# Layer 0's probability-value product in column halves, and layer 1's attention weights in another form, in a two-layer graph-attention kernel

## The chip, the cores and the metric

The kernel runs on one core of a Trainium2 chip. The core has a matrix engine (PE, whose weight loads the profile lists apart as PEld), a vector engine (DVE), an activation engine (ACT), a general engine (POOL) and a queue engine that starts transfers (SP). The engines run side by side, each through its own queue in order, and wait for each other through semaphores. The metric is the device time of one execution in microseconds (us). Three runs of the kernel before took 5745.4, 5747.46 and 5747.82 us; the median is 5747.46 us.

## The reference

The input is x of shape (8, 2048, 256), in float32, and one adjacency matrix of 2048 x 2048 integers, shared by all eight batches. Two layers follow each other, each with a residual and a layer norm around it.

Layer 0 is chunked attention with 4 heads of 64 features. For a head:

- the scores are q k^T / 8, clipped to the range -10 to 10, and -10 where the adjacency is 0;
- the softmax is taken inside each chunk of 256 keys, and not over all 2048;
- the result is the sum over the 8 chunks of probabilities times values, followed by an output projection, a residual and a layer norm. Outside it stand another residual and another layer norm.

Layer 1 is graph attention with 4 heads of 64 features. With Wh = h W, each node has two numbers per head, s (as the one who looks) and d (as the one who is looked at). The logit of the pair (i, j) is leaky(s_i + d_j) with slope 0.2; pairs without an edge get minus infinity; a softmax over j gives the weights, and the weighted sum of Wh goes through an elu. A residual and a layer norm end the kernel. The output is x after both layers.

Softmax does not change when a number is taken from all logits of a row. So the weights can be computed as exponentials of logits less the row's maximum, or in any form that differs from this by a factor per row.

## The kernel before

Everything lives on chip once loaded. Four slots of 128 x 4096 float32 hold, in turn, a batch's nodes, its transposed features, its queries and its keys; the next batch moves on by one slot, and its x is loaded into the slot of the transposed features (L81 issues it, SP's queue carries it) while layer 0 works. The adjacency is read once, in 16 blocks of rows. DVE makes a 0/1 block of each (L140), PE transposes it (L145), DVE writes `clipT` from it as +80 or -80 in int8 (L146), and ACT writes `edgeT` as 0 or 1 in uint8 (L149). In both, partitions are the nodes looked at, j.

A batch runs through `attention0`, `close0` and `attention1`.

`attention0` transposes the nodes (L157, copies L164 and L166), projects queries and keys (L188, copies L197 on DVE and L199 on ACT) and values (L204, L211 into `vaug`). `vaug` has 65 columns per head: 64 features and a column of ones (set at L200), so that a product with it also gives the sum of the weights. Then it loops over 2 pairs of heads and 4 chunks of 512 queries, here called a block, and inside over the 8 chunks of 256 keys. Such a key chunk is:

- `scores`: for each of its 2 tiles of 128 keys PE forms `ps` for the two heads (L234), keys on partitions, 512 queries along the free dimension. DVE clips with one pass that also applies the mask (L241: maximum with -80, minimum with `clipT`), and ACT takes the exponential of an eighth of it (L249), into `pr`.
- the product (L265): for each head of the pair, each of 4 groups of 128 queries and each of the 2 key tiles, PE loads 128 x 128 of `pr` as weights and streams the 65 columns of `vaug`, and accumulates over the two key tiles in `pc`.
- the division: DVE takes the reciprocal of the last column (L273) and multiplies (L274), and POOL adds the chunk to `acc` (L276).

The scores of chunk c+1 are issued ahead of the product of chunk c. At the end of a block, PE transposes `acc` (L280).

`close0` projects the output (L299) and does two layer norms on DVE, with POOL for the inverse square root (L177).

`attention1` transposes again, projects to Wh and to s and d in one product (`pw`, L343; ACT copies to `vaug`, L350; DVE copies to `sd`, L351). It then splits the exponential: with m the largest d of a head over all nodes, exp(leaky(s + d) - c) is, up to a factor of the row, exp(d - m) times max(exp(0.8 (s + m)), exp(-0.8 (d - m))). Both factors are numbers per node. So ACT takes exponentials of 64 numbers per partition (L371 to L373), POOL scales `vaug` by exp(d - m), ones column included (L375, L378), and a head needs one row vector over i, broadcast to all partitions: `row_of` builds it by PE transposes of a broadcast column (L328) and ACT copies (L331), four of 512 each. Per tile of 128 nodes j (16 a head), DVE then makes the whole weight tile of 128 x 2048 in one pass (L387): maximum of the row with a number per partition, times `edgeT`. PE multiplies it as weights, in halves of 64 columns of the array, with `vaug` (L393), into the bank pair `pa`. An epilogue per head copies `pa` (L404), divides (L410, L411, POOL L413), and does elu and residual (L416, L418, L419). The final layer norm and the store (L426, L429) end the batch.

A tile framework places the waits and orders each engine's queue by its own priorities; the order is fixed when the program is built. The pool `wk` has three buffers of 8 KB per partition, which `araw`, `ab`, `pr`, `tmp`, `e` and `o` share in turn. In PSUM, `psA` has two buffers of two banks (`ps`, `pa`), `psC` two (`pc`) and `psM` two (all else).

Of the kernel before, what the change touches and what calls it, by code (L numbers as in the profile page):

```python
# [8 lines left out]
F32 = mybir.dt.float32  # L9
BF16 = mybir.dt.bfloat16  # L10
I32 = mybir.dt.int32
I8 = mybir.dt.int8
U8 = mybir.dt.uint8
AF = mybir.ActivationFunctionType
ALU = mybir.AluOpType
AX = mybir.AxisListType

P = 128
# [4 lines left out]
def adj_resnorm_kernel(  # L23
# [33 lines left out]
    FAR = 100.0  # L57
# [13 lines left out]
    edgeT = big.tile([P, NT, N], U8, tag="edgeT", name="edgeT")  # L71
# [5 lines left out]
    def feats(s):  # L77
        return slots[s].rearrange("p (c n) -> p c n", n=N)
# [52 lines left out]

    nhalf = consts.tile([P, 4], F32, tag="nhalf", name="nhalf")
# [3 lines left out]
    for t in range(NT):  # L136
# [3 lines left out]
        nc.vector.tensor_scalar(ab, araw, 0, None, ALU.not_equal)  # L140
        for g in range(NT // 8):
# [7 lines left out]
            nc.scalar.copy(edgeT[:, 8 * g : 8 * g + 8, t * P : (t + 1) * P], pm)  # L149
# [30 lines left out]
    def attention0(b, xs, xt, qs, ks):  # L180
# [19 lines left out]
        nc.gpsimd.memset(vaug[:, :, :, D:D1], 1.0)  # L200
# [19 lines left out]
        for hp in range(HP):  # L220
            for q in range(NCH):
# [31 lines left out]
                for c in range(N // CHUNK):  # L253
# [7 lines left out]
                    for k in range(2):  # L261
                        pc = psC.tile([P, QT, D1], F32, tag="psC", name="pc")
                        for i in range(QT):
                            for u in range(KT):
                                nc.tensor.matmul(  # L265
                                    pc[:, i, :],
                                    lhsT=pr[:, u, k, i * P : (i + 1) * P],
                                    rhs=vaug[:, KT * c + u, 2 * hp + k, :],
                                    start=(u == 0),
                                    stop=(u == KT - 1),  # L270
                                )
# [61 lines left out]
    def attention1(b, xs, ts, us):  # L333

# [18 lines left out]
        top = small.tile([P, H], F32, tag="top", name="top")  # L355
        nc.vector.tensor_reduce(top, d, AX.X, ALU.max)
        pt = psM.tile([P, CH], F32, tag="psM", name="pt")
        nc.tensor.transpose(pt[:H, :P], top, identf)
        most = small.tile([H, 1], F32, tag="most", name="most")
        nc.vector.tensor_reduce(most, pt[:H, :P], AX.X, ALU.max)  # L360
        pb = psM.tile([P, CH], F32, tag="psM", name="pb")
        nc.tensor.matmul(pb[:, :H], lhsT=most.to_broadcast([H, P]), rhs=identf[:H, :H], start=True, stop=True)
        nc.vector.tensor_copy(top, pb[:, :H])
        topb = top.unsqueeze(2).to_broadcast([P, H, NT])
        nc.vector.tensor_sub(d, d, topb)
        nc.vector.tensor_add(s, s, topb)
        nc.vector.tensor_scalar(d, d, -FAR, None, ALU.max)
        nc.vector.tensor_scalar(s, s, FAR, None, ALU.min)
        ed = small.tile([P, H, NT], F32, tag="ed", name="ed", bufs=1)
        gd = small.tile([P, H, NT], F32, tag="gd", name="gd", bufs=1)  # L370
        nc.scalar.activation(ed, d, AF.Exp)  # L371
        nc.scalar.activation(gd, d, AF.Exp, scale=SLOPE - 1.0)
        nc.scalar.activation(s, s, AF.Exp, scale=1.0 - SLOPE)  # L373
        for t in range(NT):
            nc.gpsimd.tensor_mul(  # L375
                vaug[:, t, :, :D], vaug[:, t, :, :D], ed[:, :, t : t + 1].to_broadcast([P, H, D])
            )
        nc.gpsimd.tensor_copy(vaug[:, :, :, D], ed.rearrange("p h t -> p t h"))  # L378

        for h in range(H):  # L380
            srow = feats(ts if h % 2 else us)[:, h // 2, :]
            row_of(s[:, h, :], srow)

            pa = [psA.tile([P, 2, CH], F32, tag="psA", name=f"pa{k}") for k in range(2)]
            for t in range(NT):
                e = wkp.tile([P, N], F32, tag="wk", name="e")
                nc.vector.scalar_tensor_tensor(  # L387
                    e, srow, gd[:, h, t : t + 1], edgeT[:, t, :], op0=ALU.max, op1=ALU.mult
                )
                for i in range(NT):  # L390
                    bank, k = pa[i // 8][:, i // 4 % 2, :], i % 4
                    for z in range(2):
                        nc.tensor.matmul(  # L393
# [86 lines left out]
```

## Time and profile before

| What | Value |
|---|---|
| Median of the runs | 5747.46 us |
| The profiled execution's own time | 5745.4 us |
| Its span, first to last instruction | 5743.2 us |
| Mean granted clock of the matrix engine | 0.944 |
| Batch period (first `pw`, L343, of batch 0 to that of batch 1: 599.85 to 1304.24) | 704.4 us |
| Busy: PE, PEld, DVE, ACT, POOL | 86, 67, 66, 25, 19% |

The page's first part gives each engine's busy time and its share of the span. Its chain of work is followed back from the last instruction, at each step to what released it; the shares by engine say who set the end. A group of instructions is one line, engine, operation and tile; after the count come its total busy time and the mean of one, and behind the second bar the time that its engine stood idle just before it and who ended that. Matrix instructions overlap each other, so the mean of one is longer than the group's busy time over its count. In float32 one matmul of the program leaves two records in the trace, and counts of PE are counts of records. The timeline lists start, duration, engine, line and tile in order of time.

### The profile page before, as it was taken

What the parts mean: (1) busy time and instruction counts of PE and PEld (TensorE: products, weight loads), DVE (VectorE), ACT (ScalarE), POOL (GpSimd) and SP (SyncE); (2) the same over time, 40 slices, a digit from 0 to 9 for tenths busy, and PEclk for the clock granted to TensorE, in tenths of its full rate; (3) what the DMA queues carried; (4) which work ended last, traced back from release to release, by engine and by line L of the source; (5) the groups of instructions that cost most, each with busy time, mean ns of one, the idle gap of its engine ahead of it and who ended that gap; (6) DMA issues with size and microseconds to landing.
All of it is one profiled execution on the core that took longest, in us unless ns stands there. A gap on an engine that the chain in (4) does not pass through costs nothing.

```text
span 5743.2 us, 125328 instructions
## 1 busy us (share of the span) xinstructions
PE 4961.7 (86%) x56856; PEld 3875.7 (67%) x56856; DVE 3787.4 (66%) x5776; ACT 1426.5 (25%) x1657; POOL 1070.8 (19%) x825
## 2 busy tenths in 40 slices
PE   5998789978899788997889968899688996899967
PEld 3776667767677576775767758677586775767756
DVE  4656775567755686555865559655595556955569
ACT  2332113321133211332113320233102331123310
POOL 0112201131011311112111131111301113111131
PEclk9999899988999899998999979999799997999989
DMA  4000000000000000000000000000000000000000
GB/s 147 15 1 1 2 31 1 1 1 3 31 1 1 1 3 31 1 1 1 3 31 1 1 1 3 30 1 1 1 3 30 1 1 1 3 15 1 1 1 17
DMA packets 39010, 60.45 MB, mean 11 GB/s; under 512 B 1616, under 2 KB 36432, under 8 KB 36432
## 3 DMA queue, kind: packets, MB, share of 16 engines
q1 hardware_dynamic: 35712, 50.34, 2.6%
q8 instruction: 448, 7.34, 0.5%
q10 hardware_dynamic: 2768, 2.10, 0.1%
q14 instruction: 82, 0.67, 0.0%
HBM read 35.65 MB, written 16.78 MB: 9 GB/s over the span
## 4 chain that ended last, share of the span: by engine, by line
PE 68%; DVE 21%; POOL 7%; issue 3%; ACT 1%; DMA 0%; POOLq 0%; ACTq 0%; DVEq 0%
PE pc L265 33%; PE ps L234 17%; DVE e L387 10%; PE pa L393 8%; PE pp L188 4%; POOL vaug L375 2%; PE pw L343 2%; PE pv L204 2%; POOL acc L276 1%; POOL hh L413 1%; DVE pr L241 1%; DVE tmp L310 1%; DVE tmp L313 1%; PE pt L280 1%; PE pt L157 1%
## 5 line engine op out<-in xcount | busy, mean ns | idle before, releaser
L265 PEld LDWEIGHTS pc<-vaug,pr 128*128 128x128 f32 x16384 | 1867.1, 192 | 382.1 <-issue 339.6
L265 PE MATMUL pc<-vaug,pr 128*128 128x65 f32 x16384 | 1936.6, 277 | 0.0
L249 ACT ACTIVATE pr<-pr 128x1024 f32<-128x1024 f32 x1024 | 1082.4, 1057 | 2069.4 <-DVE pr L241 2036.2
L241 DVE SCALAR_TENSOR_TENSOR pr<-ps,clipT 128x1024 f32<-128x1024 f32 x1024 | 1210.4, 1219 | 315.3 <-PE ps L234 308.8
L387 DVE SCALAR_TENSOR_TENSOR e<-slot,gd,edgeT 128x2048 f32<-128x2048 f32 x512 | 1195.9, 2392 | 94.5 <-PE pa L393 56.7
L393 PE MATMUL pa<-vaug,e 128*64 128x65 f32 x32768 | 1089.6, 227 | 169.8 <-DVE e L387 100.1
L393 PEld LDWEIGHTS pa<-vaug,e 128*64 128x64 f32 x32768 | 1028.1, 142 | 236.2 <-DVE e L387 156.2
L234 PE MATMUL ps<-slot,slot 64*128 64x512 f32 x4096 | 1106.2, 620 | 29.3 <-DVE pr L241 29.3
L276 POOL TENSOR_TENSOR acc<-acc,part 128x512 f32<-128x512 f32 x448 | 568.6, 1269 | 2902.6 <-DVE part L274 2902.6
L273 DVE RECIPROCAL rd<-pc 128x4 f32<-128x4 f32 x1024 | 187.3, 183 | 872.2 <-PE pc L265 872.2
L234 PEld LDWEIGHTS ps<-slot,slot 64*128 64x128 f32 x4096 | 364.9, 185 | 348.9 <-issue 135.7
L274 DVE TENSOR_TENSOR part<-pc,rd 128x256 f32<-128x256 f32 x896 | 380.3, 424 | 63.7 <-DVE rd L273 3.2
L413 POOL TENSOR_TENSOR hh<-raw,dn 128x512 f32<-128x512 f32 x64 | 123.9, 1935 | 1178.4 <-DVE dn L410 871.3
L404 ACT COPY raw<-pa 128x520 f32<-128x520 f32 x64 | 37.9, 593 | 988.5 <-PE pa L393 988.5
L299 PE MATMUL po<-wo_sb,slot 128*128 128x256 f32 x512 | 159.0, 482 | 111.5 <-DVE tmp L306 111.5
L157 PE MATMUL pt<-identf,slot 128*128 128x128 f32 x512 | 106.7, 361 | 166.4 <-DVE slot L318 87.9
L299 PEld LDWEIGHTS po<-wo_sb,slot 128*128 128x128 f32 x512 | 125.5, 251 | 143.5 <-DVE tmp L306 120.2
L157 PEld LDWEIGHTS pt<-identf,slot 128*128 128x128 f32 x512 | 76.7, 178 | 192.4 <-issue 94.8
L188 PE MATMUL pp<-slot,wq_sb 128*128 128x512 f32 x256 | 128.4, 655 | 77.6 <-DVE slot L164 68.4
L375 POOL TENSOR_TENSOR vaug<-vaug,ed 128x256 f32<-128x256 f32 x128 | 123.3, 1004 | 190.4 <-ACT ed L371 190.4
L166 ACT COPY slot<-pt 128x512 f32<-128x512 f32 x64 | 37.1, 580 | 478.6 <-PE pt L157 478.5
L188 PEld LDWEIGHTS pp<-slot,wq_sb 128*128 128x128 f32 x256 | 51.8, 210 | 149.3 <-DVE slot L164 74.2
(78 smaller groups left out, 2343.5 us busy)
## 6 DMA issues: line engine op xcount, KB each, us to landing
slot<-in_x_dram SPq DMA_DIRECT2D x8, 2048.0 KB, 8.5
araw<-in_adj_dram SPq DMA_DIRECT2D x16, 1024.0 KB, 4.8
out_dram<-o SPq DMA_DIRECT2D x32, 512.0 KB, 2.9
wq_sb<-in_wqT_dram ACTq DMA_DIRECT2D x1, 256.0 KB, 5.9
wk_sb<-in_wkT_dram ACTq DMA_DIRECT2D x1, 256.0 KB, 8.0
wv_sb<-in_wvT_dram ACTq DMA_DIRECT2D x1, 256.0 KB, 8.8
wo_sb<-in_woT_dram ACTq DMA_DIRECT2D x1, 256.0 KB, 9.7
w_sb<-in_w_dram ACTq DMA_DIRECT2D x1, 256.0 KB, 9.0
```

The source lines that it names most:

```text
L157: nc.tensor.transpose(pt[:, k * P : (k + 1) * P], src[:, q * QT + k, c * P : (c + 1) * P], identf,)
L188: nc.tensor.matmul(pp, lhsT=w[:, kc, c * P : (c + 1) * P], rhs=xT[:, kc, q * CH : (q + 1) * CH], start=(kc == 0), stop=(kc == KC - 1),)
L234: nc.tensor.matmul(ps[:, k, :], lhsT=kT[rows, hp, t * P : (t + 1) * P], rhs=qT[rows, hp, cols], start=True, stop=True,)
L241: nc.vector.scalar_tensor_tensor(pr[:, u], ps, -CLIP, clipT[:, t, cols].unsqueeze(1).to_broadcast([P, 2, CH]), op0=ALU.max, op1=ALU.min,)
L249: nc.scalar.activation(pr[:, u], pr[:, u], AF.Exp, scale=0.125)
L265: nc.tensor.matmul(pc[:, i, :], lhsT=pr[:, u, k, i * P : (i + 1) * P], rhs=vaug[:, KT * c + u, 2 * hp + k, :], start=(u == 0), stop=(u == ...
L274: nc.vector.tensor_mul(part[:, k], pc[:, :, :D], rd.to_broadcast([P, QT, D]))
L276: nc.gpsimd.tensor_add(accv, accv, part)
L299: nc.tensor.matmul(po[:, k, :], lhsT=cT[:, c, t * P : (t + 1) * P], rhs=wo_sb[:, c, :], start=(c == 0), stop=(c == KC - 1),)
L375: nc.gpsimd.tensor_mul(vaug[:, t, :, :D], vaug[:, t, :, :D], ed[:, :, t : t + 1].to_broadcast([P, H, D]))
L387: nc.vector.scalar_tensor_tensor(e, srow, gd[:, h, t : t + 1], edgeT[:, t, :], op0=ALU.max, op1=ALU.mult)
L393: nc.tensor.matmul(bank[z * D : (z + 1) * D, k * D1 : (k + 1) * D1], lhsT=e[:, i * P + z * D : i * P + (z + 1) * D], rhs=vaug[:, t, h, :], ...
```

## The change

Two things are changed, in the two layers.

In layer 0, each product of probabilities and values (L265) with 128 queries as weights is issued as two products with 64 queries, each to its own half of the partitions of `pc`, and so on its own half of the array's columns.

In layer 1 the split of the exponential is replaced by logits less each row's maximum. `vaug` is filled with ones once at the start and not scaled. Instead of `edgeT`, ACT keeps `mask`, the adjacency with the looking nodes i on partitions. For each head a row of d over j is built (`drow`), shifted to be at least 1, and for each tile of 128 nodes i one fused DVE operation multiplies it with the mask and takes the maximum along the row (L366 after the change). From s and this maximum DVE forms `gg`, so that with `s8` = 0.8 s and `d8` = -0.8 d the logit less its row's maximum is max(s8_i, d8_j) + gg_i + d_j. A head needs two rows, of `s8` and of `gg`. Per tile of nodes j DVE forms max(s8, d8) + gg (L396), then bounds it by 1e30 times `clipT`, which sends pairs without an edge far down (L400), and ACT takes the exponential with d as the bias (L401). PE multiplies with `vaug` as weights and the tile as the moving operand, in four products of 512 columns, into a transposed result of 65 x 2048 (L403). The epilogue copies it (L412), transposes it back in 16 pieces (L419), and divides and finishes in four groups on DVE, with ACT for the exponential (L422 to L431).

```diff
-    FAR = 100.0
+    FAR = 1e30
...
-    edgeT = big.tile([P, NT, N], U8, tag="edgeT", name="edgeT")
+    mask = big.tile([P, NT, N], U8, tag="mask", name="mask")
...
+    nc.gpsimd.memset(vaug, 1.0)
...
+        nc.scalar.copy(mask[:, t, :], ab)
...
-            nc.scalar.copy(edgeT[:, 8 * g : 8 * g + 8, t * P : (t + 1) * P], pm)
...
-        nc.gpsimd.memset(vaug[:, :, :, D:D1], 1.0)
...
-                                nc.tensor.matmul(
-                                    pc[:, i, :],
-                                    lhsT=pr[:, u, k, i * P : (i + 1) * P],
-                                    rhs=vaug[:, KT * c + u, 2 * hp + k, :],
-                                    start=(u == 0),
-                                    stop=(u == KT - 1),
-                                )
+                                for z in range(2):
+                                    half = slice(z * D, (z + 1) * D)
+                                    nc.tensor.matmul(
+                                        pc[half, i, :],
+                                        lhsT=pr[:, u, k, i * P + z * D : i * P + (z + 1) * D],
+                                        rhs=vaug[:, KT * c + u, 2 * hp + k, :],
+                                        start=(u == 0),
+                                        stop=(u == KT - 1),
+                                    )
...
-        top = small.tile([P, H], F32, tag="top", name="top")
...
-        nc.scalar.activation(ed, d, AF.Exp)
-        nc.scalar.activation(gd, d, AF.Exp, scale=SLOPE - 1.0)
-        nc.scalar.activation(s, s, AF.Exp, scale=1.0 - SLOPE)
-        for t in range(NT):
-            nc.gpsimd.tensor_mul(
-                vaug[:, t, :, :D], vaug[:, t, :, :D], ed[:, :, t : t + 1].to_broadcast([P, H, D])
+        most = small.tile([P, H, NT], F32, tag="most", name="most", bufs=1)
+        low = small.tile([P, H], F32, tag="low", name="low", bufs=1)
+        for h in range(H):
+            drow = wkp.tile([P, N], F32, tag="wk", name="drow")
+            row_of(d[:, h, :], drow)
+            nc.vector.tensor_reduce(low[:, h : h + 1], drow, AX.X, ALU.min)
+            nc.vector.tensor_scalar(drow, drow, low[:, h : h + 1], 1.0, ALU.subtract, ALU.add)
+            for t in range(NT):
+                scr = small.tile([P, N], BF16, tag="scr", name="scr", bufs=1)
+                nc.vector.tensor_tensor_reduce(
+                    out=scr,
+                    in0=drow,
+                    in1=mask[:, t, :],
+                    scale=1.0,
+                    scalar=0.0,
+                    op0=ALU.mult,
+                    op1=ALU.max,
+                    accum_out=most[:, h, t : t + 1],
+                )
+            nc.vector.tensor_scalar(
+                most[:, h, :], most[:, h, :], low[:, h : h + 1], -1.0, ALU.add, ALU.add
             )
-        nc.gpsimd.tensor_copy(vaug[:, :, :, D], ed.rearrange("p h t -> p t h"))
...
+        nc.vector.tensor_scalar(s8, s, 1.0 - SLOPE, None, ALU.mult)
+        nc.vector.tensor_scalar(d8, d, SLOPE - 1.0, None, ALU.mult)
+        nc.vector.tensor_add(most, most, s)
+        nc.vector.scalar_tensor_tensor(most, most, SLOPE, most, op0=ALU.mult, op1=ALU.max)
+        nc.vector.scalar_tensor_tensor(gg, s, SLOPE, most, op0=ALU.mult, op1=ALU.subtract)
...
-            srow = feats(ts if h % 2 else us)[:, h // 2, :]
-            row_of(s[:, h, :], srow)
-
+            sg = feats(ts if h % 2 else us)
+            srow, grow = sg[:, 0, :], sg[:, 1, :]
+            row_of(s8[:, h, :], srow)
+            row_of(gg[:, h, :], grow)
...
                 nc.vector.scalar_tensor_tensor(
-                    e, srow, gd[:, h, t : t + 1], edgeT[:, t, :], op0=ALU.max, op1=ALU.mult
-                )
...
+                    e, srow, d8[:, h, t : t + 1], grow, op0=ALU.max, op1=ALU.add
+                )
+
+                nc.vector.scalar_tensor_tensor(e, clipT[:, t, :], FAR, e, op0=ALU.mult, op1=ALU.min)
+                nc.scalar.activation(e, e, AF.Exp, bias=d[:, h, t : t + 1])
+                for q in range(NCH):
+                    nc.tensor.matmul(
+                        pa[q // 2][:D1, q % 2, :],
+                        lhsT=vaug[:, t, h, :],
+                        rhs=e[:, q * CH : (q + 1) * CH],
+                        start=(t == 0),
+                        stop=(t == NT - 1),
+                    )
+            hT = wkp.tile([D1, N], F32, tag="wk", name="hT")
+            for k in range(2):
                 nc.scalar.copy(
...
+                    hT[:, 2 * k * CH : 2 * (k + 1) * CH], pa[k][:D1].rearrange("p a n -> p (a n)")
+                )
+            for g in range(NT // 4):
+                ph = psM.tile([P, 4, D1], F32, tag="psM", name="ph")
+                for k in range(4):
+                    t = 4 * g + k
+                    nc.tensor.transpose(ph[:, k, :], hT[:, t * P : (t + 1) * P], identf[:D1, :D1])
...
+                nc.vector.tensor_mul(hh, ph[:, :, :D], dn.to_broadcast([P, 4, D]))
```

Lines after the change are numbered some two lines higher up to `close0`: L265 becomes L267, L273 becomes L275, L188 becomes L189, L328 and L331 (`row_of`) become L330 and L333, L157 and L164 become L158 and L165.

## The prediction, made before the changed kernel was run

> **What bounds the kernel now.** I read the page's busy times first, then its chain, then the costliest groups, then the timeline of one chunk of layer 0 and of one head of layer 1.
>
> ```profile
> PE 4961.7 (86%) x56856; PEld 3875.7 (67%) x56856; DVE 3787.4 (66%) x5776; ACT 1426.5 (25%) x1657; POOL 1070.8 (19%) x825
> ...
> PE 68%; DVE 21%; POOL 7%; issue 3%; ACT 1%; DMA 0%; POOLq 0%; ACTq 0%; DVEq 0%
> ...
> L265 PE MATMUL pc<-vaug,pr 128*128 128x65 f32 x16384 | 1936.6, 277 | 0.0
> L241 DVE SCALAR_TENSOR_TENSOR pr<-ps,clipT 128x1024 f32<-128x1024 f32 x1024 | 1210.4, 1219 | 315.3 <-PE ps L234 308.8
> L387 DVE SCALAR_TENSOR_TENSOR e<-slot,gd,edgeT 128x2048 f32<-128x2048 f32 x512 | 1195.9, 2392 | 94.5 <-PE pa L393 56.7
> L393 PE MATMUL pa<-vaug,e 128*64 128x65 f32 x32768 | 1089.6, 227 | 169.8 <-DVE e L387 100.1
> ```
>
> PE sets the end overall, but the two layers differ. A group ends in "busy us, mean ns of one", and a count is of records: a float32 matmul leaves two. L265 is 1936.6 / 16384 = 118 ns a record with a full-width weight load; L393, the same 65 moving columns on half the array's columns, is 1089.6 / 32768 = 33 ns.
>
> In the timeline one chunk of layer 0 goes like this (columns: start, duration, engine, line):
>
> ```profile
> 505.60 3.79 PE L265 MATMUL pc<-vaug,pr 128*128 128x65 f32 x32
> 507.64 0.18 DVE L273 RECIPROCAL rd<-pc 128x4 f32<-128x4 f32 x1 [0.35 <-PE pc L265]
> 507.93 0.43 DVE L274 TENSOR_TENSOR part<-pc,rd 128x256 f32<-128x256 f32 x1
> 509.32 1.99 PE L234 MATMUL ps<-slot,slot 64*128 64x512 f32 x8
> 509.43 0.18 DVE L273 RECIPROCAL rd<-pc 128x4 f32<-128x4 f32 x1 [1.07 <-PE pc L265]
> ```
>
> PE has no hole: 3.72 us of pc, then 1.91 us of ps, a period of 5.63 us, while the window of that period shows DVE 3.56 and ACT 2.11 us. PE is the bound here. In a head of layer 1 DVE is:
>
> ```profile
> 622.02 7.83 DVE L387 SCALAR_TENSOR_TENSOR e<-slot,gd,edgeT 128x2048 f32<-128x2048 f32 x3 [4.46 <-ACT slot L331]
> 633.51 12.70 PE L393 MATMUL pa<-vaug,e 128*64 128x65 f32 x384 [8.21 <-POOL vaug L378]
> 682.96 27.23 DVE L387 SCALAR_TENSOR_TENSOR e<-slot,gd,edgeT 128x2048 f32<-128x2048 f32 x12
> 703.45 2.09 PE L393 MATMUL pa<-vaug,e 128*64 128x65 f32 x64 [0.17 <-DVE e L387]
> ```
>
> Twelve passes back to back take 27.23 us, 2.27 us each; PE needs 2.12 us per tile (12.70 / 6) and waits 0.17 to 0.18 us for each.
>
> [...]
>
> **The change, part by part.** Units are one batch (8 of them), 8 layer-0 blocks (2 head pairs x 4 query chunks) of 8 key chunks, and 4 heads of 16 tiles.
>
> *Layer 0, halves.* Per key chunk 32 records of 118 ns become 64. Nearest row: L393, 12.70 / 384 = 33.1 ns, so 2.12 us for 3.72. ps stays, so PE's period is 1.91 + 2.12 = 4.03 us. DVE's own needs are 3.56 us busy and some 0.25 us of dependent gaps, so PE still leads, by little. The probabilities are done in time: ACT ends the next chunk's exponentials about 4.7 us after its ps begin, its pc starts at 4.03 + 1.91. A block takes 48.58 us now (435.74 to 484.32). Eight chunks give 12.8 us; I take off 0.8 for the seam between blocks, where DVE's four passes and POOL's last sum were covered by the longer pc. 12.0 x 64 = 768 us saved. Bounds: 640 (DVE leads, period 4.35) to 820 (nothing lost).
>
> *Layer 1, what goes.* From the first pw (599.85) to the next batch's first pp (797.32) is 197.5 us, and from there to 857.0, just ahead of that batch's first pc (858.51), 59.7; together 257.2. In it are POOL's scaling of vaug (15.4), one DVE pass per tile, and PE's halves.
>
> *Layer 1, what comes*, on DVE, in order of its queue:
> 1. pw as now, 15.5; then the first row: 4 transposes and a copy, four times, as 618.07 to 622.0 now: 3.9.
> 2. Row maxima: per head a reduction of 2048 (estimate 2.28 from L125's 416 ns at 256, at 1.04 ns an element), a subtract of 2048 (1.22, L140), small ones; 15 for four. Then 64 fused passes. Each is a pass like L387 (2.34) and a readout of the accumulator (a tiny operation, 0.15 as L176), and each waits for the one in front: 2.5 us, 160. POOL, ACT and PE have nothing beside it: all of it is path. Bounds 2.35 to 2.7; half rate, 4.65, is a rival.
> 3. gg's small operations and its row: 5.1, DVE idle.
> 4. The weights: two passes per tile in place of one. 2.34 + 2.27, of which the second reads what the first wrote; such a pair shows a gap of 0.04 (rd to part at 509.43) where independent ones overlap by 0.07. 4.62 x 64 = 296. Under it ACT's exponential runs (1.06 at 1024 elements, L249, so 1.91 at 2048[...]) and PE's four matmuls of 512 columns: L188's run at 107.18 is 27.47 us for 64 records, 0.43 each, 3.43 per tile. Both fit under 4.62, and a tile of e is free after about 10.3 us where three buffers allow 13.9. Uncovered, PE would cost only if its clock falls (below).
> 5. Seams. DVE's queue holds a head's whole epilogue ahead of the next head's first pass, and PE's and ACT's queues hold the next head's two rows behind the epilogue. So after the last pass: exponential 2.1, matmuls to the first copy 2.0, copy of 1024 (1.03), transposes 1.1; then the 24 epilogue operations of DVE, whose fourth exponential ends 13.1 us after the last pass; then seven row copies on ACT, 5.7 to 6.3 us (625.7 - 618.75 for eight now). 19.5 between heads, three times: 58.5. Bounds 14 and 23.
> 6. The last head's epilogue, norms on DVE (four groups at 3.7 us, as 5727.01 to 5730.70) and the next batch's four transposed copies queued behind these; those transposes can't start before, since both halves of that slot carry rows now. 28 us, where 6.4 passes now from the last pass (790.92). The next projections then meet no norms and take what the first batch took, 48.5 (105 to about 153.7, ahead of its first pc at 154.28).
>
> Sum: 15.5 + 3.9 + 160 + 15 + 5.1 + 296 + 58.5 + 28 + 48.5 = 630.5 for 257.2: 373.3 more, x 8 = 2986 us.
>
> *Setup.* 16 mask copies of 2048 on ACT for 32 of edgeT at 1012 ns, one memset of vaug on POOL: nothing; PE's transposes and DVE's passes of the adjacency (period 4.61 at 87.86 to 92.48) hide them. Uncovered, some 15 us. DMAs are the same, on the same queues.
>
> Total against the profiled execution: 5743.2 - 768 + 2986 = 7961 span, with its 2.2 us around it 7963. Its 5745.4 is the lowest of the three; their median is 2 higher. Forecast 7963.
>
> **Rivals.**
> - *Half rate of the fused pass.* 2.15 us more x 512 = 1100: 9060.[...] 8 in 100.
> - *PE becomes the bound of the weights.* PE stands idle for the 175 us of maxima, and at 46% busy it was granted 0.68 (540 to 600, 27.54 of 59.85 us). At half clock its 3.43 would be 6.9 us a tile, 2.2 over DVE: 64 x 2.2 x 8 = 1130, so 9090. Against it: it would be 74% busy, and layer 1 holds 0.95 now. 4 in 100.
> - *The halves gain little in layer 0*: alternating tile shapes with ps every chunk, or DVE at the lead, leave below 300 us of the 768: 8500 to 8730. Against it, ps already has another shape than pc, and DVE's 3.8 is under 5.63. 4 in 100.
> - *Not slower.* The one way is that the added passes cost little: 8 x (c - 257.2) = 768 needs c = 353.2 a batch; all that isn't the three passes is 174.5, which leaves 178.7 / 64 = 2.79 us for three passes, 0.93 each. It decides at 0.93 us, and the quickest 2048-element pass on the page with only one tensor to read takes 1.22 (L140). 1 in 100.
>
> **How the numbers follow.** My sum has 83 in 100. Its ends: fused pass 2.35, pair 4.54, seams 14, tail 22, layer 0 at 820 give about 7620; fused 2.7, pair 4.75, seams 23, tail 32, layer 0 at 640 give about 8300. All these ends together are unlikely; 7660 to 8380 holds all but 3 of the 83, with room for a seam or a clock that I mis-sized upward. That is 8 in 10. The half rate, the clock and the lost halves lie outside. This kernel can be told from no change at about 0.2%, 11.5 us: slower by more than that has 0.985, within it 0.005, faster 0.01.
>
> **What would show it.** Layer 0's period per chunk: 4.03 us, pc records at 33 ns, and DVE and PE both near 95% busy. Fused passes at 2.3 to 2.4 us each with a readout after each; PE idle beside them for 175 us a batch. L396 and L400 at 4.6 us a pair with ACT at 2 us and PE at 3.4 us a tile under them. About 19 us without a long DVE pass between heads. DVE, not PE, heads the chain, with well over half. The forecast fails if a fused pass takes over 4 us, if PE's clock in the weights is near a half, or if the seams are hidden after all.

## The result, and the profile after

The changed kernel takes 7855.78 us, the median of four runs (7854.82 to 7859.9), beside 5747.64 us for the kernel before on the same chip: a ratio of 1.3669, with a 95% interval of 1.3645 to 1.3692. The forecast was 7963 us in 7660 to 8380, so the sign was right and the time 1.4% too high. The profiled execution took 7854.82 us; its span is 7853.0 us, 2109.8 more than before, and the mean granted clock of the matrix engine fell from 0.944 to 0.839.

The page of the changed kernel, in its busy times, its chain and its costliest groups:

```profile
PE 5282.2 (67%) x46080; PEld 2779.2 (35%) x46080; DVE 6220.3 (79%) x7904; ACT 2635.4 (34%) x2449; POOL 824.0 (10%) x618
...
DVE 45%; PE 43%; ACT 5%; issue 4%; POOL 3%; DMA 0%; ACTq 0%; DVEq 0%; POOLq 0%
...
L403 PE MATMUL pa<-e,vaug 128*65 128x512 f32 x4096 | 2011.8, 649 | 659.6 <-ACT e L401 652.0
...
L396 DVE SCALAR_TENSOR_TENSOR e<-slot,d 128x2048 f32<-128x2048 f32 x512 | 1191.3, 2346 | 238.7 <-ACT slot L333 141.5
...
L366 DVE CUSTOM_DVE_ANT_0 scr<-drow,mask 128x2048 bf16<-128x2048 f32 x512 | 1172.5, 2290 | 15.2
L400 DVE SCALAR_TENSOR_TENSOR e<-clipT,e 128x2048 f32<-128x2048 int8 x512 | 1160.7, 2287 | 8.8
...
L267 PE MATMUL pc<-vaug,pr 128*64 128x65 f32 x32768 | 1082.2, 224 | 24.6 <-DVE rd L275 22.8
```

Three DVE groups of 512 passes, 1161 to 1191 us each, stand where L387 stood with 1196: the two added ones, L366 and L400, are 2333 us of DVE's busy time. On the other side, L267 has twice the records of L265 and takes 1082.2 us for 1936.6.

In the timeline a key chunk of layer 0 now reads (start, duration, engine, line):

```profile
351.71 2.09 PE L267 MATMUL pc<-vaug,pr 128*64 128x65 f32 x64
353.73 1.99 PE L234 MATMUL ps<-slot,slot 64*128 64x512 f32 x8
354.97 2.36 DVE L241 SCALAR_TENSOR_TENSOR pr<-ps,clipT 128x1024 f32<-128x1024 f32 x2 [0.41 <-PE ps L234]
355.64 0.74 PE L267 MATMUL pc<-vaug,pr 128*64 128x65 f32 x18
```

From one start of pc to the next it is 3.93 us (351.71 to 355.64) where it was 5.63: 2.02 for 64 records, 31.6 ns each, and 1.91 for ps. PE is busy in all of it, and DVE waits 0.41 us for ps: PE still bounds the chunk. A block, from one transpose of `acc` to the next, takes 35.57 us for 48.58.

In the phase of the row maxima DVE is alone:

```profile
534.80 2.29 DVE L366 CUSTOM_DVE_ANT_0 scr<-drow,mask 128x2048 bf16<-128x2048 f32 x1
537.02 0.08 DVE L366 DVE_READ_ACCUMULATOR2_ANT most<- 128x1 f32 x1
537.14 2.29 DVE L366 CUSTOM_DVE_ANT_0 scr<-drow,mask 128x2048 bf16<-128x2048 f32 x1
```

A fused pass and its read-out come every 2.34 us. Between two heads of the weights DVE stands still twice:

```profile
755.63 2.29 DVE L400 SCALAR_TENSOR_TENSOR e<-clipT,e 128x2048 f32<-128x2048 int8 x1
765.80 0.16 DVE L422 TENSOR_SCALAR dn<-ph 128x4 f32<-128x4 f32 x1 [7.87 <-PE ph L419]
...
776.71 4.61 DVE L396 SCALAR_TENSOR_TENSOR e<-slot,d 128x2048 f32<-128x2048 f32 x2 [4.39 <-ACT slot L333]
```

Here it waits 7.87 us for the first transposed sums, has 6.3 us of epilogue, small gaps, and waits 4.39 us for the next head's rows: 18.8 us without a long pass.

Term by term, for one batch, in us (means over the batches; the times in brackets are batch 0's, whose first `pw` starts at 496.93):

| Term | forecast | measured |
|---|---|---|
| Layer 0 with its close, against before | -96 | -102.4 (342.9 from first pc to first pw, for 445.3) |
| pw and the first row, to the first reduction (515.54) | 19.4 | 18.6 |
| row maxima | 175 | 163.1 |
| gg and its row | 5.1 | 5.0 |
| weights, four heads | 296 | 303.1 |
| three seams | 58.5 | 55.2 |
| tail, to the next pp (1042.65 to 1076.07: 33.4) | 28 | 31.0 |
| next projections, to the first pc (1124.41: 48.3) | 48.5 | 49.0 |
| all of the last seven rows; before | 630.5; 257.2 | 625.0; 258.3 |

Over the kernel, layer 0 gave 819 us (768 forecast) and layer 1 took 2929 (2986 forecast): 51 and 58 make up the 108 us by which the sum was too high.

### The profile page after: what moved, and what is told of

The parts are those of the page before. It is cut to its first block, busy times and chain, and to the rows that moved or that the text cites. A ratio compares the mean times of both kernels' runs of the same rounds, so it can differ in the third digit from the quotient of the medians.

```text
span 7853.0 us, 107020 instructions
## 1 busy us (share of the span) xinstructions
PE 5282.2 (67%) x46080; PEld 2779.2 (35%) x46080; DVE 6220.3 (79%) x7904; ACT 2635.4 (34%) x2449; POOL 824.0 (10%) x618
## 4 chain that ended last, share of the span: by engine, by line
DVE 45%; PE 43%; ACT 5%; issue 4%; POOL 3%; DMA 0%; ACTq 0%; DVEq 0%; POOLq 0%
DVE scr L366 15%; PE pc L267 12%; PE ps L234 11%; DVE e L396 11%; PE pa L403 10%; DVE e L400 7%; ACT e L401 4%; PE pp L189 3%; DVE pr L241 3%; PE pb L330 2%; PE pw L344 2%; PE pv L204 1%; POOL acc L278 1%; DVE low L362 1%; DVE tmp L312 1%
## 5 line engine op out<-in xcount | busy, mean ns | idle before, releaser
L403 PE MATMUL pa<-e,vaug 128*65 128x512 f32 x4096 | 2011.8, 649 | 659.6 <-ACT e L401 652.0
L401 ACT ACTIVATE e<-e,sd 128x2048 f32<-128x2048 f32 x512 | 1025.4, 2003 | 1468.7 <-DVE e L400 1468.7
L249 ACT ACTIVATE pr<-pr 128x1024 f32<-128x1024 f32 x1024 | 1083.0, 1058 | 1259.5 <-DVE pr L241 1226.9
L396 DVE SCALAR_TENSOR_TENSOR e<-slot,d 128x2048 f32<-128x2048 f32 x512 | 1191.3, 2346 | 238.7 <-ACT slot L333 141.5
L403 PEld LDWEIGHTS pa<-e,vaug 128*65 128x65 f32 x4096 | 589.4, 149 | 2062.0 <-issue 1178.0
L366 DVE CUSTOM_DVE_ANT_0 scr<-drow,mask 128x2048 bf16<-128x2048 f32 x512 | 1172.5, 2290 | 15.2
L400 DVE SCALAR_TENSOR_TENSOR e<-clipT,e 128x2048 f32<-128x2048 int8 x512 | 1160.7, 2287 | 8.8
L267 PEld LDWEIGHTS pc<-vaug,pr 128*64 128x64 f32 x32768 | 1004.0, 138 | 414.8 <-issue 362.3
L267 PE MATMUL pc<-vaug,pr 128*64 128x65 f32 x32768 | 1082.2, 224 | 24.6 <-DVE rd L275 22.8
L330 PE MATMUL pb<-identf,gg 128*128 128x128 f32 x512 | 97.0, 349 | 892.1 <-DVE gg L386 887.9
L333 ACT COPY slot<-pb 128x512 f32<-128x512 f32 x256 | 146.5, 585 | 938.0 <-PE pb L330 936.9
L330 PEld LDWEIGHTS pb<-identf,gg 128*128 128x128 f32 x512 | 73.8, 179 | 914.2 <-issue 889.9
L330 PE MATMUL pb<-identf,sd 128*128 128x128 f32 x512 | 85.3, 302 | 342.0 <-ACT drow L333 336.0
L275 DVE RECIPROCAL rd<-pc 128x4 f32<-128x4 f32 x1024 | 178.0, 174 | 150.4 <-PE pc L267 150.4
L158 PE MATMUL pt<-identf,slot 128*128 128x128 f32 x512 | 128.6, 422 | 240.1 <-DVE slot L320 87.9
```

The source lines that it names most:

```text
L249: nc.scalar.activation(pr[:, u], pr[:, u], AF.Exp, scale=0.125)
L267: nc.tensor.matmul(pc[half, i, :], lhsT=pr[:, u, k, i * P + z * D : i * P + (z + 1) * D], rhs=vaug[:, KT * c + u, 2 * hp + k, :], start=(u ...
L330: nc.tensor.transpose(pb[:, k * P : (k + 1) * P], col[:, t : t + 1].to_broadcast([P, P]), identf)
L366: nc.vector.tensor_tensor_reduce(out=scr, in0=drow, in1=mask[:, t, :], scale=1.0, scalar=0.0, op0=ALU.mult, op1=ALU.max, accum_out=most[:, ...
L396: nc.vector.scalar_tensor_tensor(e, srow, d8[:, h, t : t + 1], grow, op0=ALU.max, op1=ALU.add)
L400: nc.vector.scalar_tensor_tensor(e, clipT[:, t, :], FAR, e, op0=ALU.mult, op1=ALU.min)
```

## Experiments

**The halves alone.** The first part of the change in the kernel before:

```diff
-                                nc.tensor.matmul(
-                                    pc[:, i, :],
-                                    lhsT=pr[:, u, k, i * P : (i + 1) * P],
...
+                                for z in range(2):
+                                    half = slice(z * D, (z + 1) * D)
+                                    nc.tensor.matmul(
+                                        pc[half, i, :],
+                                        lhsT=pr[:, u, k, i * P + z * D : i * P + (z + 1) * D],
```

> The kernel before with one part of the change alone: layer 0's product in halves; layer 1 as before. Theory A, the two parts of the change do not touch each other: in the trace after, the first pw of a batch comes 102.7 us earlier (497.14 against 599.85), so 8 x 102.7 = 822 us go, 4926 us. Theory B, the parts help each other (layer 1 after leaves PE idle, and PE then has full clock in the next batch's layer 0): the halves alone then meet a busier PE, the clock falls below 1.00 in layer 0, and the gain is clearly less, my own term of 768 or under it: 4980 us or more.

4932.4 us, ratio 0.8584 (0.857 to 0.8599), so 813.6 us less than before. In the changed kernel layer 0 gave 819 us; so the parts of the change add up to within 6 us, and theory B is out. A block takes 35.57 us here too.

**One half after the other.**

```diff
-                        for i in range(QT):
-                            for u in range(KT):
-                                for z in range(2):
+                        for z in range(2):
+                            for i in range(QT):
+                                for u in range(KT):
```

> As the halves alone, but with the loop over the two halves outermost: 16 matmuls for queries 0 to 63 of each 128, all on one half of the columns, then 16 on the other half. Same instructions, same operands, other order. Theory A, the gain comes from neighbouring matmuls on different halves of the columns whose weight loads and streams run side by side: in this order neighbours share a half, so a record goes from 31.6 ns towards the 118 ns of the full width or at least to 60, pc from 2.02 us to 3.8 or more for 64 records, a chunk to 5.7 us or more; about 1.8 x 8 x 64 = 900 us over the halves alone, 5800 us and perhaps more than the kernel before. Theory B, a load of 64 columns is simply so much shorter than one of 128 that order plays no part: same as the halves alone, 4926 us.

5551.25 us, 619 more than the halves alone. The timeline:

```profile
352.00 3.41 PE L267 MATMUL pc<-vaug,pr 128*64 128x65 f32 x64
355.35 1.99 PE L234 MATMUL ps<-slot,slot 64*128 64x512 f32 x8
```

64 records now take 3.35 us, 52 ns each, with the same instructions and operands. So the order matters, but my lower bound of 60 ns was too high: two records of 64 columns one after the other (104 ns) are a little cheaper than one of 128 (118). Of the 1.70 us that a chunk gains, 1.33 belong to neighbours on different halves, 0.37 to the shape. The starts of the single records in the two traces show the pairing (medians): with the halves alone a record on the other half starts 7 ns after its neighbour, and the next pair follows 52 ns later. One half after the other, a record starts 58 ns after the one before it, whether both sum into the same place of `pc` or not, so repeated sums into one place are not what costs; only where the half changes, after every 16 records (8 products), do some start 2 to 6 ns apart.

**Quarters.** `range(4)` and 32 queries in place of `range(2)` and 64.

> As the halves alone, but in quarters of 32 queries, each on its own 32 columns of the array: 128 records for each chunk's pc in place of 64. Theory A, neighbours run side by side, and more tiles give more of it: a record goes to about 16 ns, pc at or under 2.0 us, and the chunk stays at 3.9 or falls to DVE's limit of about 3.8: 4860 to 4930 us. Theory B, at 31.6 ns a record PE is at the pace at which it can issue: the record stays at about 32 ns, pc takes 4.1 us, the chunk 6.0: (6.0 - 3.93) x 512 = 1060 us over the halves alone, about 5990 us.

4973.78 us, 41 more than the halves alone: theory A's record and chunk, but neither theory's time. Its group and its timeline:

```profile
L267 PE MATMUL pc<-vaug,pr 128*32 128x65 f32 x65536 | 1087.9, 221 | 106.5 <-issue 78.4
```

```profile
387.49 2.02 PE L267 MATMUL pc<-vaug,pr 128*32 128x65 f32 x128
389.44 1.99 PE L234 MATMUL ps<-slot,slot 64*128 64x512 f32 x8
```

A record does go to 15.2 ns (1.95 us for 128), so PE was not at the pace of its issue, and a chunk to 3.87 us. But twice the records at half the time give next to nothing: a chunk's product takes 1.95 us for 2.02, and 512 chunks at 0.06 are 31 us. And PE now has holes ahead of these products, 78.4 us in all, in which it waits for nothing that the profile shows; blocks take from 34.84 to 40.28 us, with the halves 35.57 for the most part. The program's instruction transfers grew from 9.44 to 13.63 MB; whether the holes have to do with that, no run shows.

**Less DVE and POOL in layer 0.** In the halves alone:

```diff
-                        nc.vector.tensor_mul(part[:, k], pc[:, :, :D], rd.to_broadcast([P, QT, D]))
+                        nc.vector.tensor_mul(
+                            part[:, k, : QT // 2 if c else QT],
...
-                        nc.gpsimd.tensor_add(accv, accv, part)
+                        nc.gpsimd.tensor_add(accv[:, :, : QT // 2], accv[:, :, : QT // 2], part[:, :, : QT // 2])
```

> As the halves alone, with work of DVE and POOL left out: for key chunks 1 to 7 only half of each scaled product is formed and summed (the multiplication of pc by rd and POOL's sum, queries of two of the four tiles left out). PE's work is unchanged. It takes 2 x about 0.21 us from DVE's 3.4 us busy in a chunk. Theory A, PE bounds layer 0 after the halves (it has 3.93 of 3.93 us busy in a chunk): less than 30 us change from the halves alone. Theory B, DVE's chain of passes sets the pace and PE's records only stretch to fill it: 0.3 to 0.4 us a chunk go, 150 to 200 us in all.

4868.19 us, 64 less: between the two. The trace splits it. Starts of pc are still 3.93 us apart (347.60, 351.53): inside a block PE bounds, as theory A has it. But a block is 34.76 us for 35.57, and that 0.81 lies at its end. PE waits there for POOL's last sum before it can transpose `acc`, 1.09 us with the halves alone and 0.41 here; and ahead of the last chunk's product it waits until DVE has read the buffer of `pc` that this product is to fill, 0.36 us and 0.23.

**The last sum on DVE.**

```diff
-                        nc.gpsimd.tensor_add(accv, accv, part)
+                        eng = nc.vector if c == N // CHUNK - 1 else nc.gpsimd
+                        eng.tensor_add(accv, accv, part)
```

> The run with the halves alone, with the sum of a block's last key chunk on DVE in place of POOL. It asks what holds the 0.6 us that a block of layer 0 loses at its end: with less work of DVE and POOL left in a block, 64 us went, and of that PE's wait for POOL's last sum ahead of the transposes of acc fell from 1.09 to 0.42 us. Theory A, the last sum is on the path: on DVE 512 elements take about 0.7 us (0.42 at 256) for POOL's 1.27 and a hand-over less, so the transposes start 0.5 to 0.76 us earlier: 32 to 49 us less than the halves alone, 4885 to 4900 us. Theory B, DVE is the path there: its sum stands ahead of the next block's passes over ps, which then come later by what PE gains: within 10 us of the halves alone, 4932.

4892.38 us, ratio 0.8516 (0.8502 to 0.853), 40 less than the halves alone. A block takes 34.96 us, the sum 0.69 for POOL's 1.27, and PE's wait ahead of the transposes is 61.3 us in all for 101.4, which is the gain:

```profile
359.26 0.65 PE L283 MATMUL pt<-identf,acc 128*128 128x128 f32 x4 [0.48 <-DVE acc L279]
```

Theory A holds: the last sum is on the path. But this is not what a block loses by the change. In the kernel before, PE waits for POOL's last sum as well (90.6 us in all; one such wait is the first line below). What is new is the wait ahead of the last product, which the kernel before doesn't have (second and third line, from the changed kernel, at one block's end):

```profile
490.25 0.66 PE L280 MATMUL pt<-identf,acc 128*128 128x128 f32 x4 [1.08 <-POOL acc L276]
```

```profile
358.09 0.34 PE L267 MATMUL pc<-vaug,pr 128*64 128x65 f32 x4 [0.36 <-DVE rd L275]
...
363.53 0.66 PE L282 MATMUL pt<-identf,acc 128*128 128x128 f32 x4 [1.09 <-POOL acc L278]
```

Of the versions that leave no work out, this is the fastest that ran here: it keeps the first part of the change and leaves layer 1 as before.

**The rows ahead.** In the changed kernel:

```diff
-        for h in range(H):
+        def rows(h):
             sg = feats(ts if h % 2 else us)
...
+        ahead = rows(0)
+        for h in range(H):
+            srow, grow = ahead
+            if h + 1 < H:
+                ahead = rows(h + 1)
```

> The changed kernel with one thing moved: the two rows of head h + 1 are built (transposes on PE, copies on ACT) ahead of head h's passes, not behind head h's epilogue; their slot is free, since heads alternate between two. Theory A, my item 5: a seam between heads is serial work in queue order, and the rows are its last part, 4.39 us in which DVE waits for the last row copy (757.92 to 776.71 in all). They vanish under the passes: 24 seams x 4.4 = 105 us less than the changed kernel, about 7750 us; a seam goes from 18.8 to 14.4 us. Theory B, DVE would have to wait for something else at that place, PE's clock or the matmuls of the head: under 30 us less.

7647.08 us, ratio 1.3297 (1.3275 to 1.332): 209 less than the changed kernel, twice what theory A had. DVE's waits, first of the changed kernel, then with the rows ahead (what waits, for what, total, times, longest):

```profile
DVE dn L422 <- PE ph L419: 234.6, 32, 9.2
...
DVE e L396 <- ACT slot L333: 141.5, 32, 4.8
...
DVE e L396 <- PE pa L403: 86.2, 71, 2.1
```

```profile
DVE dn L428 <- PE ph L425: 138.2, 56, 6.1
DVE e L402 <- PE pa L409: 107.8, 77, 4.3
...
DVE e L402 <- ACT slot L333: 33.6, 8, 4.2
```

The wait for rows lost 107.9 us, which is my 105. Another 96.4 came off the other wait of the seam, and 21.6 came back as waits for a buffer; the rest of the 209 lies in no wait that this view lists. Once the rows are issued early, the framework's fixed order puts the next head's first passes into the epilogue: one ahead of it, and the next between the first divisions, at 767.37.

```profile
763.36 2.35 DVE L402 SCALAR_TENSOR_TENSOR e<-slot,d 128x2048 f32<-128x2048 f32 x1 [4.28 <-PE pa L409]
```

So the order that I had taken for a fixed rule of the queue came with the late rows.

**Two tiles ahead.**

```diff
+            if h + 1 < H:
+                early = {t: weights(h + 1, t) for t in range(2)}
             for g in range(NT // 4):
```

> As the run with the rows ahead, and besides the weights of the next head's first two tiles (two passes on DVE and one exponential on ACT each) are issued ahead of the epilogue. Theory A: DVE has these 9.25 us of passes where it now waits. The buffer of tile 14 comes free at about 761.5, so its first pass runs from there to 766.2, the second to 770.8, the epilogue's 6.3 us follow, and tile 2 starts at about 777 where it now starts 28 us after the last pass (18.8 + 9.25 = 28.05 against 19.2): 24 x 8.9 = 212 us less than the changed kernel, about 7640. Theory B, the exponentials ahead of the epilogue's small ones on ACT and the matmuls behind its transposes on PE only move the wait to the first tiles of the next head: no less than the run with the rows ahead, about 7750 or more.

7620.32 us, ratio 1.3253 (1.3233 to 1.3273): 235 below the changed kernel, close to the 212, but only 27 below the run with the rows ahead. Theory A's total was met by other steps than its own: passes already ran in the seam with the rows alone, and the two tiles, priced at 107 beyond the rows' 105, gave 27.

**Half of the products.** Even tiles' products left out:

```diff
-                for q in range(NCH):
+                for q in range(NCH if t % 2 else 0):
```

> The changed kernel with half of layer 1's products of weights and values left out: only odd tiles enter PE's sum; DVE's and ACT's work on all tiles stays. PE then needs 1.97 us a tile for 3.93. Theory A, PE is covered by DVE's 4.63 us a tile except where it shows as a wait: 86 us in which DVE waits for PE to free a buffer of e, and at each head's end what of the last two tiles' 7.86 us of matmuls runs beyond the last exponential plus one tile, about 1.6 us, 32 x 1.6 = 51: 137 us less, about 7720 us. Theory B, the weights are PE's after all (the clock that is granted in them is 0.89, and the chain runs along PE for a good part of a head): the passes come closer together within a head, below 4.5 us a pair, and far more than 200 us go. Theory C, with PE idle for longer the clock falls further and the epilogues, the norms and the next projections take longer: less than 60 us go.

7752.44 us, 103 less, between theories A and C. From first to last pass the 32 heads take 2289.3 us for 2424.9, 135.6 less. That is near theory A's 137 by chance: A had 86 of it inside the heads and 51 at their ends. Inside the heads DVE's waits for PE (86.2) and for the exponential (10.7) are gone, and about 30 us come from the passes themselves; at the ends nothing was gained, for the seams grew from 441.6 to 470.2, theory C's part. The windows of the passes of the first head show PE's side (columns: window, length, then busy us of PE, PEld, DVE, ACT and POOL, then the granted clock):

```profile
685.20:756.72 71.52, 39.79 (x56) 10.53 (x56) 71.52 (x32) 30.03 (x15) 0.00 (x0) 0.71 0.00 0
```

For the changed kernel:

```profile
683.56:757.92 74.36, 54.15 (x111) 15.89 (x112) 72.42 (x32) 30.05 (x15) 0.00 (x0) 0.89 0.00 0
```

With half the work PE's busy time is still 73% of the changed kernel's in this head (39.79 us for 54.15) and 66% over all 32 (36.9 us for 55.8), at a granted clock of 0.71 for 0.89 here, and of 0.76 for 0.87 over all. The low clock then reaches into the seams. A tile's eight records take 3.65 us at a granted clock of 1.00 (746.58 in the changed kernel); behind the second head's last exponential they took 6.47 here, at 0.56. And DVE's wait for the first transposed sums rose from 234.6 us to 261.9, 27 of the 28.6:

```profile
849.08 6.47 PE L403 MATMUL pa<-e,vaug 128*65 128x512 f32 x8 [3.58 <-ACT e L401]
```

```profile
DVE dn L422 <- PE ph L419: 261.9, 32, 9.1
```

DVE has no hole left in a head: 71.52 us for 16 tiles, 4.47 a tile, is what the two passes cost by themselves. Theory B had this sign, under 4.5 us a pair, but not the 200 us with it.

**Four buffers.**

```diff
-    wkp = ctx.enter_context(tc.tile_pool(name="wk", bufs=3))
+    wkp = ctx.enter_context(tc.tile_pool(name="wk", bufs=4))
...
+            scr = wkp.tile([P, N], BF16, tag="wk", name="scr")
             for t in range(NT):
-                scr = small.tile([P, N], BF16, tag="scr", name="scr", bufs=1)
```

> The changed kernel with four buffers of 8 KB in the pool of e in place of three (the fused pass's scratch output lies in that pool too, to make room). Theory A, the 86 us in which DVE waits for PE to free a buffer are a matter of buffering: PE needs 3.93 us a tile at the clock it gets and DVE 4.63, so PE catches up later in the head: 60 to 90 us less than the changed kernel, about 7780. Theory B, PE's last tile does not come earlier by it, so the wait only moves to the head's end, where DVE waits for the transposed sums: under 20 us less.

7672.89 us, ratio 1.3355 (1.3335 to 1.3374): 183 less, twice theory A's. The heads lost 136.3 us, to 71.52 each, the same floor as with half of the products, though PE has all of its work here; so either cure, less work for PE or one more buffer, removes the waits. DVE no longer waits for a buffer of e, and its passes come in pairs (two of L396, two of L400) all through a head, so that no pass follows the one whose result it reads, as half of the 512 second passes do in the changed kernel; the two groups are 25 us less busy. The maxima lost 52.2 us, 156.5 a batch for 163.1, which I had not meant to touch. Two runs follow that up.

**The scratch, once a head.** In the changed kernel, the line of `scr` moved ahead of the loop over t.

> The changed kernel with one edit: the scratch output of the fused pass is taken from its pool once a head, not once a pass (same buffer, three buffers for e as before). In the run with four buffers 183 us went where 60 to 90 were expected; in its profile the heads are 136.3 us shorter in all, and the phases of the maxima 52.2 us, with a fused pass every 2.213 us in place of 2.337. Theory A, the second part is the scratch: taking a buffer anew makes each pass wait for the release of the pass in front, 0.124 us: 512 x 0.124 = 63, of which 52 showed; about 52 us less than the changed kernel, 7804. Theory B, it came with the fourth buffer (a row of the next head that is there earlier): the pass stays at 2.337 us, under 10 us less.

7880.04 us, ratio 1.3715 (1.3692 to 1.3738), 24 more than the changed kernel; a fused pass still comes every 2.34 us. Theory A fell. The 24 are mainly in the heads (2443.0 us for 2424.9), which the edit doesn't touch. They go with PE's clock: 15 of the 32 heads take over 77 us here, 7 in the changed kernel, and in each of these the granted clock is 0.82 to 0.85, while the others, at 76.1 or less, have 0.87 to 0.89. Why other heads have the low clock here, is open.

**Two scratches.**

```diff
-                scr = small.tile([P, N], BF16, tag="scr", name="scr", bufs=1)
+                scr = small.tile([P, N], BF16, tag="scr", name="scr", bufs=2)
```

> The changed kernel with two scratch buffers for the fused pass in place of one, taken anew in each pass as before; three buffers for e. Taking the one scratch once a head changed nothing in a fused pass (2.337 us still), so the 2.213 us of the run with four buffers came from something else. Theory A: there two scratches were live, the passes of two heads took turns, and neighbours wrote to different buffers; what costs 0.124 us is that a pass waits for the pass in front to have written the buffer that both use. Then two buffers do the same: 2.213 us a pass, 512 x 0.124 = 63 us at most and 52 as seen there, so 50 to 65 us less than the changed kernel, about 7800. Theory B, the wait is on something else that two heads do not share (the row, the accumulator's read-out into the same small tile): still 2.337 us and under 10 us less.

7800.31 us, ratio 1.357 (1.3548 to 1.3593), 55 less. In the timeline:

```profile
534.72 2.29 DVE L366 CUSTOM_DVE_ANT_0 scr<-drow,mask 128x2048 bf16<-128x2048 f32 x1
536.93 0.08 DVE L366 DVE_READ_ACCUMULATOR2_ANT most<- 128x1 f32 x1
536.93 2.29 DVE L366 CUSTOM_DVE_ANT_0 scr<-drow,mask 128x2048 bf16<-128x2048 f32 x1
```

A pass every 2.21 us, and the next one starts with the read-out and not 0.12 us after it. Theory A holds: a pass that writes the buffer which the pass in front wrote waits for it, on one engine too. In both traces each such pass waits for a semaphore that the read-outs raise. With one buffer it starts some 0.03 us after the end of the read-out in front. So by its timing the cost is that of a wait which the framework places; what two passes into one buffer would cost without it, no run shows.

**Half of the maxima.**

```diff
+        nc.gpsimd.memset(most, 1.0)
...
-            for t in range(NT):
+            for t in range(0, NT, 2):
```

> The changed kernel with half of the row maxima left out: the fused multiply-and-maximum runs for the even tiles only, the others' maxima are set to 1.0. Theory A, my item 2: DVE alone carries the phase and nothing runs under it, so 32 passes x 2.337 us x 8 batches = 598 us go, 7257 us, to within 10. Theory B, part of the phase hides work that shows when it is shorter (copies, the clock, row copies that wait): clearly less than 598, 500 or under. Theory C, the idle phase costs PE its clock in what follows: more than 598 goes, since the weights and the tail behind it then run at a higher clock.

7274.94 us, 581 less. The phases themselves are 88.4 us for 163.1, 597.6 in all, so nothing runs under them. 17 us come back elsewhere, more than the 10 I allowed, and 14 of them are in the heads (2439.1 us for 2424.9): 12 of the 32 take over 77 us, where 7 did.

## Why the prediction was right, point by point

The mechanism was right in both layers: PE's product set layer 0's pace, and three passes of DVE set layer 1's. That the total is off by only 1.4% is partly luck: over the kernel the forecast of the maxima was 95 us too high and that of the weights 57 too low, and within the weights two errors cancel.

- *Layer 0, halves*: the mechanism was right, the term mis-sized by 51 us. I took the new record from a group's busy time over its count (33.1 ns, and the page shows 33.0 again), but in a run of 64 a start-to-start distance counts, 31.6 ns; the old 3.72 us was such a distance. So the period is 3.93 and not 4.03. The loss at a block's end is real and was 0.6 us, not 0.8 (8 x 1.70 = 13.6 against 13.01). Its place was half right: the traces put it at the wait for DVE's reading of `pc` ahead of the last product (0.36 us, none before), and not at POOL's last sum, for which PE waits about as long in the kernel before (1.08 us and 1.09). No run takes DVE's part away alone. "DVE and PE both near 95% busy" was wrong for DVE: 3.38 of 3.93 us, 86%.
- *Item 2, the maxima*: all of it is path, as half of the maxima showed. The fused pass took 2.34 us, just below my lower bound of 2.35: I counted the read-out at 0.15, and it is 0.08 and overlaps. 0.16 x 512 = 82 of the 95 us. Without its read-out the pass, which the trace lists as a custom operation, takes 2.29 us for 2048 elements of a float32 row and a uint8 mask, where L387, with the same kinds of sources, has a median of 2.34. So the half rate did not occur; the trace of the kernel before had no such pass for it or against it, and the rival that was worth 1100 us fell. The reduction of 2048 took the 2.28 us of my estimate (L362, 2281 ns; with L125's 416 at 256 that is 1.04 ns an element).
- *Item 4, the weights*: 296 forecast, 303.1 measured, two errors of opposite sign. The two passes alone are 4.47 us a tile, not 4.62; I priced each second pass as one that follows its own source, and half of them are interleaved in pairs. And PE did cost: without its hold on the buffers the heads lose 136 us, 86 of them waits for it and most of the rest passes that come in pairs. I had allowed 13.9 us for a tile of e against 10.3 needed. What failed is the PE price at full clock: 3.43 us a tile became 3.93 at a granted 0.87, and tiles reach ACT at uneven distances, two and two. ACT's exponential, 1.91 us by my estimate from L249, took 2.00. The rival that PE becomes the bound stayed small.
- *Item 5, the seams*: 18.4 us on average for 19.5, but not by the steps. From the last exponential to PE's first result it is 3.85 us for my 2.0 in the seam shown, since PE is behind by more than one tile there (12 records are left, a tile has 8); the epilogue and the rows are shorter. The queues do hold the order that I gave, but it isn't fixed: with the rows ahead the passes move into the epilogue by themselves.
- *Item 6, the tail*: 31.0 for 28 (33.4 in batch 0), the same late PE result (6.2 to 9.2 us of waiting ahead of the last epilogue) beside a clock of 0.65 in batch 0; their shares were not separated. The next projections were right to 0.5 us.
- *The chain*: I expected DVE ahead "with well over half". It has 45% and PE 43%, since the 343 us a batch of layer 0 are still PE's.
- *Not slower* was excluded by the passes: three of them take 6.8 us a tile, and it would have needed 2.79.
- *The sums of the ends*: the upper ends named add up to 8376 us, not to about 8300, so the range had no room above them; and the rival of the lost halves begins at 7963 + 468 = 8431, not at 8500. Neither decided anything.

## What to carry to other kernels

A change that helps PE where PE bounds (here 814 us) can still come with a larger loss: two added passes over every element, on the engine that bounds the other stage, cost 2929 us with the seams and the tail around them, and no repair of seams and buffers that was tried, each alone, got back more than 235 of it. Price a record in a burst by the distance of starts, price PE at the clock that it gets in a stage with as many holes (0.87 in these heads, 0.76 with half of their products), and let neighbouring instructions alternate, between halves of the array on PE (31.6 ns a record for 52) and between output buffers on DVE (2.21 us a pass for 2.34). Before you call a seam serial by queue order, ask which late input put the order there.

## What the runs showed of the hardware that I had not expected

- The same 64 records take 2.02 us in alternating column halves, where neighbours start 7 ns apart, and 3.35 us one half after the other, where they start 58 ns apart; quarters go to 15.2 ns a record but gain 0.07 us a chunk.
- Successive DVE passes into one output buffer, with the wait that the framework places between them, start 0.12 us later each than passes into two buffers in turn (2.34 and 2.21 us).
- Halving PE's work in layer 1's heads lowered its granted clock there from 0.87 to 0.76, its busy time fell to 66% and not to a half, and the seams after the heads grew from 441.6 to 470.2 us.
